# Layer 1's attention with its causal sum taken of the tokens, and one product for values and output

## The chip, the cores and the metric

The kernel runs on one core of one Trainium2 chip. The metric is device time in microseconds (us) of one execution, lower is better. TensorE is called PE below, VectorE DVE, ScalarE ACT, GpSimd POOL, and SyncE's queue SP.

## The reference, cut to what matters

The program is a small vision tower on 32 images of 256 tokens with 256 features: a tokenizer, layer 0 (gated attention, then a token-choosing feed-forward part), and layer 1 (the attention below, then a feed-forward part with heads and experts). The change touches only layer 1's attention and the preparation of its weights. Its input is a layer norm of the residual stream.

```python
def _L1_attn_ref(x, Wk1, bk1, Wk2, bk2, Wq1, bq1, Wq2, bq2, Wv, bv, ln_w, ln_b, Wo, bo):
    ...
    def encode(W1, b1, W2, b2):
        h = jax.nn.gelu(x @ W1 + b1, approximate=False)
        return jnp.tanh(h @ W2 + b2)
    key_phase = encode(Wk1, bk1, Wk2, bk2) * freq * jnp.pi
    query_phase = encode(Wq1, bq1, Wq2, bq2) * freq * jnp.pi
    key_phasor = jnp.cos(key_phase) + 1j * jnp.sin(key_phase)
    query_conj = jnp.cos(query_phase) - 1j * jnp.sin(query_phase)
    V = (x @ Wv + bv).astype(jnp.complex64)
    bound = key_phasor[..., None] * V[:, :, None, :]
    memory = jnp.cumsum(bound, axis=1)
    retrieved = jnp.real(jnp.sum(memory * query_conj[..., None], axis=2))
    positions = jnp.arange(1, Ll + 1, dtype=jnp.float32)
    retrieved = retrieved / jnp.sqrt(positions * K)[None, :, None]
    mu = jnp.mean(retrieved, axis=-1, keepdims=True)
    var = jnp.var(retrieved, axis=-1, keepdims=True)
    normed = (retrieved - mu) / jnp.sqrt(var + 1e-05) * ln_w + ln_b
    return x + normed @ Wo + bo
...
h = h + _L1_attn_ref(_layernorm(h, axis=-1), L1_attn_Wk1, ...)
```

The cumulative sum is the same as a causal match matrix (token against token, from the phases) times the values. Everything is float32.

## The kernel before, in words

The kernel goes through five stages, A to E: tokenizer (A), layer 0's attention (B), layer 0's feed-forward part (C), layer 1's attention (D), layer 1's feed-forward part (E). The residual stream of all images stays in SBUF, as 32 tiles `H[b]` of 128 partitions x 2 token blocks x 256 features. The eight PSUM banks are one pool; `bank()` takes the next of them, and a product into a bank waits until the bank's last reader has read it.

Stage D works on pairs of images, 16 pairs. Each pair goes through these steps, and three steps of time separate one pair from the next, so several pairs are under way at once:

- `norm`: two image tiles `dx` by DVE (line 172), four of them in turn; POOL adds `dx` and the row `add_row` to `H` (lines 623 and 624).
- `turn`: eight PE transposes of `dx` into two banks; ACT copies the first bank into `dxT`, DVE the second (`copy_split`, lines 191 and 193).
- `hidden`: for keys and for queries, four products of `wk1` or `wq1` with `dxT`, 512 columns each; ACT's gelu reads the bank (line 722).
- `phases`: the second layer into one bank, tanh (ACT), then range reduction on DVE into `dz`.
- `values_d`: eight products of `dxT` with `wv`, 256 columns each; DVE adds the bias row into `dv` (line 757).
- `match`: the sine (ACT), eight products of `dz`, and DVE multiplies with the causal weights into `dat` (line 777).
- `memory`: six products of `dat` with `dv`, 256 columns each; ACT copies them into `dr` (line 789); DVE takes mean and variance (`bn_stats` and `bn_aggr`, lines 792 and 793), and POOL makes the reciprocal deviation `d_rs` (`pow_rstd`, lines 146 and 147).
- `turn_back`: eight PE transposes of `dr`, copied into `drT` by ACT and DVE.
- `output`: eight products of `drT` with `wo1`, 256 columns each; DVE scales by `d_rs` and adds to `H` (line 813), and takes the statistics of `H` that stage E needs (lines 121 and 122).

In each step of time the steps that are due are written out in this order:

```python
ORDER = ((1, turn), (7, output), (4, match), (2, hidden), (5, memory), (3, phases), (6, turn_back),
         (3, values_d), (0, norm))
for t in range(3 * (B // 2 - 1) + 8):
```

So in the steady state PE's queue repeats, for each pair's period: match, hidden, memory, phases, turn_back, values_d, turn, output. A scheduler may move instructions against this order when the program is built, and each engine then works through its own queue in order. At step 21 `residuals` runs once: stage E's first products on images 0 to 3.

`prepare` runs once, in stage C, after its ninth step. It centres `wv` and the bias row (the reference's subtraction of the mean), makes `add_row` from `ln_b`, `Wo` and `bo`, multiplies `wo1` by `ln_w`, and makes stage E's weights. Its products stand in PE's queue between two of stage C's groups.

Of the kernel before, what the change touches and what calls it, by code (L numbers as in the profile page):

```python
# [29 lines left out]
F32 = mybir.dt.float32  # L33
AF = mybir.ActivationFunctionType
# [5 lines left out]
P = 128  # L40
# [38 lines left out]
def vit_tower(tc, a, out):  # L79
# [14 lines left out]
    def bank():  # L94
        return ppool.tile([P, 512], F32, name="bank", tag="bank")

    def col(name, i=0):
        c = COLS[name][0] + i
        return cols[:, c : c + 1]

    def load_rows(pool, name, at, n, eng=nc.scalar):

        t = pool.tile([P, n], F32, name=name)
        eng.dma_start(t, a[name].partition_broadcast(P))
        return lambda x: t[:, at[x][0] : at[x][0] + at[x][1]]

    def load(pool, name, eng=nc.scalar):
        t = pool.tile(list(a[name].shape), F32, name=f"w_{name}")
        eng.dma_start(t, a[name])
        return t  # L110
# [4 lines left out]
    def over(ap, shape, axis):  # L115
        return ap.unsqueeze(axis).to_broadcast(shape)
# [330 lines left out]
    pm = passing.enter_context(tc.tile_pool(name="e_made", bufs=1, side="right", reuse_waits="tile"))  # L447
    wk1, wq1 = load(pwd, "wk1", nc.sync), load(pwd, "wq1", nc.sync)
    wk2, wq2 = load(pwd, "wk2", nc.sync), load(pwd, "wq2", nc.sync)
    wv, wo1 = load(pwd, "wv1", nc.sync), load(pwd, "wo1", nc.sync)  # L450
    row_d = load_rows(pwd, "rows_d", ROWS_D, N_ROWS_D)
    causal = load(pwd, "causal_scaled", nc.sync)

    add_row = pwd.tile([P, D], F32, name="add_row")
    row_e = load_rows(pwe, "rows_e", ROWS_E, N_ROWS_E)
    hl, tri = load(pwe, "hl", nc.sync), load(pwe, "tri", nc.sync)
    cen, fg = load(pwe, "centre", nc.sync), load(pwe, "fg", nc.sync)
# [44 lines left out]
    def prepare():  # L502


        for w, g in ((wv, 2), (row_d("bv").unsqueeze(1), 1)):
            m = spool.tile([P, g], F32, name="d_mean", tag=f"d_mean{g}", bufs=1)
            nc.vector.tensor_reduce(m, w, AX.X, ALU.add)
            nc.vector.tensor_scalar(m, m, 1.0 / D, None, ALU.mult)
            nc.vector.tensor_tensor(w, w, over(m, [P, g, D], 2), ALU.subtract)
        p = bank()  # L510
        for k in range(2):
            mm(p[:, 0:D], col("ln_b", k).to_broadcast([P, P]), wo1[:, k, :], k == 0, k == 1)
        nc.vector.tensor_tensor(add_row, p[:, 0:D], row_d("bo"), ALU.add)
        for k in range(2):
            nc.vector.tensor_scalar(wo1[:, k, :], wo1[:, k, :], col("ln_w", k), None, ALU.mult)

        nc.gpsimd.memset(ones_row, 0.0)
        for o in (NE, EC + NE, 2 * EC + HD + NE, 3 * EC + HD + NE):
# [97 lines left out]
    def norm_d(b0, s, pool, name, bufs):  # L616
        s.xs = []
        for j in range(2):
            x = pool.tile([P, NC, D], F32, name=name, bufs=bufs)
            normed(x, b0 + j, st_d)  # L620
            s.xs.append(x)
            h = H[b0 + j]
            nc.gpsimd.tensor_tensor(h, h, x, ALU.add)
            nc.gpsimd.tensor_tensor(h, h, over(add_row, [P, NC, D], 1), ALU.add)
# [77 lines left out]
    with (  # L702
# [10 lines left out]

        def hidden(b0, s):
            s.g = []
            for i, (w, bias) in enumerate(((wk1, "bk1"), (wq1, "bq1"))):
                g = p2.tile([P, 2, 2 * N], F32, name=f"dg{i}")
                for m in range(2):
                    p = bank()
                    for k in range(2):  # L720
                        mm(p, w[:, k, m * P : (m + 1) * P], s.xT[:, k, :], k == 0, k == 1)
                    nc.scalar.activation(g[:, m, :], p, AF.Gelu, bias=col(bias, m))
                s.g.append(g)

        def phases(b0, s):
# [19 lines left out]
            nc.vector.tensor_scalar(n, z, MAGIC, MAGIC, ALU.add, ALU.subtract)  # L745
            nc.vector.tensor_sub(z, z, n)

        def values_d(b0, s):
            s.v = []
            for j in range(2):  # L750
                p = bank()
                for c in range(NC):
                    for k in range(2):
                        o = j * N + c * P
                        mm(p[:, c * D : (c + 1) * D], s.xT[:, k, o : o + P], wv[:, k, :], k == 0, k == 1)
                v = p8.tile([P, NC, D], F32, name="dv", bufs=6)
                nc.vector.tensor_tensor(
                    v, p.rearrange("p (c d) -> p c d", c=NC), over(row_d("bv"), [P, NC, D], 1), ALU.add
                )
                s.v.append(v)  # L760

        def match(b0, s):
            z = s.z.rearrange("p i n -> p (i n)")
            nc.scalar.activation(z, z, AF.Sin, scale=TWO_PI)
# [13 lines left out]
                s.t.append(t)  # L778

        def memory(b0, s):  # L780
            s.r = []
            s.st = spool.tile([P, 2 * NC, 2], F32, name="d_st")
            for j in range(2):
                t, v, p = s.t[j], s.v[j], bank()
                mm(p[:, 0:D], t[:, 0:P], v[:, 0, :])
                mm(p[:, D : 2 * D], t[:, P:N], v[:, 0, :], True, False)
                mm(p[:, D : 2 * D], t[:, N : N + P], v[:, 1, :], False, True)
                r = p8.tile([P, NC, D], F32, name="dr", bufs=4)
                nc.scalar.copy(r.rearrange("p c d -> p (c d)"), p)
                for c in range(NC):  # L790
                    six = spool.tile([P, 6], F32, name="six")
                    nc.vector.bn_stats(six, r[:, c, :])
                    nc.vector.bn_aggr(s.st[:, j * NC + c, :], six)
                s.r.append(r)
            s.rs = spool.tile([P, 2 * NC], F32, name="d_rs")
            pow_rstd(s.rs, s.st[:, :, 1])

        def turn_back(b0, s):
            s.rT = p2.tile([P, 2, 2 * N], F32, name="drT")
            transposed(s.rT, s.r, copy_split)  # L800

        def output(b0, s):
            for j in range(2):
                b = b0 + j
                p = bank()
                for c in range(NC):
                    for k in range(2):
                        o = j * N + c * P
                        mm(p[:, c * D : (c + 1) * D], s.rT[:, k, o : o + P], wo1[:, k, :], k == 0, k == 1)
                st, rs, i = at(st_e, b)  # L810
                for c in range(NC):
                    h, q = H[b][:, c, :], j * NC + c
                    nc.vector.scalar_tensor_tensor(
                        h, p[:, c * D : (c + 1) * D], s.rs[:, q : q + 1], h, ALU.mult, ALU.add
                    )
                    stats(st, i, c, h)
            pow_rstd_of(st_e, b0, 2)

        ORDER = ((1, turn), (7, output), (4, match), (2, hidden), (5, memory), (3, phases), (6, turn_back),
                 (3, values_d), (0, norm))
        for t in range(3 * (B // 2 - 1) + 8):
            if 1 <= t <= 3:
                step_c(END_C + t - 1)
            for at_step, do in ORDER:
                u, r = divmod(t - at_step, 3)
                if r == 0 and 0 <= u < B // 2:
                    do(2 * u, pairs[u])
            if t == 21:  # L830
                residuals(p2)
# [709 lines left out]
```

## Time and profile before

| what | value |
|---|---|
| three runs | 2065.7, 2072.34, 2075.61 us; median 2072.34 us |
| the profiled execution | 2072.35 us, of which the span from the first to the last instruction is 2070.5 us |
| mean granted PE clock | 0.978 of full speed |
| PE busy | 1984.3 us, 96% of the span |
| PE's weight loads | 1438.7 us, 69% |
| DVE busy | 1319.8 us, 64% |
| ACT busy | 829.6 us, 40% |
| POOL busy | 738.7 us, 36% |
| stage D | about 966 to 1340 us of the span |
| `prepare` on PE | 779.8 to 786.2 us |

The page divides the span in 40 slices of 51.8 us; stage D is slices 19 to 26. In the trace a float32 product of PE stands as two records, a transpose as one. Such records overlap: a 256-column record lasts 379 ns, but the next one starts 0.21 us after it. So starts are compared with starts here, not lengths.

### The profile page before, as it was taken

How to read it: one execution, taken by the hardware profiler on the slowest of the kernel's cores; microseconds unless marked ns; L12 is line 12 of the kernel's file. 1: busy time of each engine (PE TensorE's matmuls, PEld its weight loads, DVE VectorE, ACT ScalarE, POOL GpSimd, SP SyncE). 2: the span in 40 equal slices, each digit the busy share in tenths (PEclk: the TensorE clock that was granted, in tenths of full speed). 3: DMA queues.
4: the chain of work that ended last, by engine and by line, in shares of the span. 5: the costliest groups of instructions: out<-in, count | busy, mean ns of one | idle time of the engine just before them, and what ended most of it. 6: DMA issues, size and time to landing. Idle time of an engine off the chain costs nothing.

```text
span 2070.5 us, 38268 instructions
## 1 busy us (share of the span) xinstructions
PE 1984.3 (96%) x15406; PEld 1438.7 (69%) x15406; DVE 1319.8 (64%) x3589; ACT 829.6 (40%) x1569; POOL 738.7 (36%) x691
## 2 busy tenths in 40 slices
PE   8999999999999899998999999999999999999994
PEld 7886676666756656665666676677777777777772
DVE  3333557667575643335665565547888888888886
ACT  0001322222221021221433443367777777777762
POOL 2222224334242343336342332103444343444443
PEclk9999999999999999999999999989999999999996
DMA  8540000000000322212000000001222222121222
GB/s 273 153 145 0 1 0 21 13 19 18 13 21 11 127 81 72 74 53 58 1 1 1 1 1 1 1 19 35 53 48 56 50 49 57 43 61 45 58 50 55
DMA packets 69207, 95.12 MB, mean 46 GB/s; under 512 B 8480, under 2 KB 50592, under 8 KB 68640
## 3 DMA queue, kind: packets, MB, share of 16 engines
q1 hardware_dynamic: 62160, 74.33, 12.9%
q0 software_dynamic: 6144, 16.79, 2.8%
q8 instruction: 123, 2.02, 0.4%
q10 hardware_dynamic: 720, 1.50, 0.2%
q14 instruction: 60, 0.49, 0.1%
HBM read 46.45 MB, written 20.97 MB: 33 GB/s over the span
## 4 chain that ended last, share of the span: by engine, by line
PE 70%; DVE 20%; ACT 6%; DMA 2%; issue 2%; POOL 1%; SPq 0%; DVEq 0%; ACTq 0%; POOLq 0%
PE bank L113 66%; DVE bank L932 4%; ACT et L934 2%; PE bank L186 2%; DVE ranges L1025 1%; DVE two L1017 1%; ACT g L892 1%; DVE fout L1095 1%; DVE fout L1091 1%; DVE ev L905 1%; ACT foT L1078 1%; DVE er L1019 1%; DVE enorm L1066 1%; PE bank L583 1%; DVE ey L1058 1%
## 5 line engine op out<-in xcount | busy, mean ns | idle before, releaser
L113 PEld LDWEIGHTS bank<-ev,et 128*64 128x64 f32 x6144 | 198.2, 137 | 34.0 <-ACT et L934 21.7
L934 ACT ACTIVATE et<-bank 128x512 f32<-128x512 f32 x384 | 202.4, 598 | 34.8 <-DVE bank L932 34.1
L113 PE MATMUL bank<-ev,et 128*64 128x74 f32 (+1 forms) x6144 | 211.2, 226 | 0.0
L1012 POOL TENSOR_TENSOR eo<-eo,gate 128x1024 f32<-128x1024 f32 x64 | 131.5, 2074 | 204.7 <-DVE gate L1009 156.7
L932 DVE TENSOR_TENSOR bank<-bank,w_tri 128x256 f32<-128x256 f32 (+1 forms) x384 | 172.0, 515 | 30.2 <-PE bank L113 29.5
L113 PE MATMUL bank<-g,sx 64*128 64x512 f32 (+1 forms) x512 | 186.6, 506 | 1.4 <-ACT g L892 1.4
L113 PE MATMUL bank<-g,sw 64*128 64x512 f32 (+1 forms) x512 | 185.5, 507 | 1.4 <-DVE ev L905 1.4
L113 PE MATMUL bank<-w_tokW,patch 128*128 128x256 f32 x768 | 169.0, 384 | 9.3 <-DMA w_tokW<-in_tokW_dram 9.3
L113 PEld LDWEIGHTS bank<-w_tokW,patch 128*128 128x128 f32 x768 | 148.0, 193 | 30.0 <-issue 9.3
L113 PE MATMUL bank<-bxT,w_wuv 128*128 128x512 f32 x320 | 147.9, 601 | 4.3 <-ACT bxT L191 4.0
L191 ACT COPY bxT<-bank 128x512 f32<-128x512 f32 x16 | 9.4, 585 | 339.2 <-PE bank L186 339.2
L964 POOL TENSOR_TENSOR hv<-hv,minus_half 128x8 f32<-128x8 f32 x64 | 119.5, 1868 | 5.3
L950 ACT COPY eo<-bank 128x286 f32<-128x286 f32 x256 | 97.2, 422 | 48.7 <-PE bank L113 40.9
L113 PE MATMUL bank<-w_w,hT 128*128 128x256 f32 x512 | 114.5, 383 | 0.0
L963 POOL TENSOR_SCALAR hv<-ranges 128x8 f32<-128x8 f32 x64 | 38.8, 606 | 210.8 <-DVE ranges L1025 210.8
L113 PE MATMUL bank<-xsel,w_w 128*128 128x512 f32 x256 | 113.5, 600 | 0.0
L113 PE MATMUL bank<-attn,bv 128*128 128x256 f32 x512 | 113.3, 379 | 0.0
L113 PE MATMUL bank<-w_wo,gT 128*128 128x256 f32 x512 | 113.1, 379 | 0.0
L113 PE MATMUL bank<-w_wuv,bxT 128*128 128x512 f32 x256 | 112.5, 592 | 0.0
L113 PEld LDWEIGHTS bank<-attn,bv 128*128 128x128 f32 x512 | 97.1, 190 | 19.5 <-issue 6.7
L113 PEld LDWEIGHTS bank<-w_w,hT 128*128 128x128 f32 x512 | 97.9, 192 | 16.8 <-issue 3.8
L113 PEld LDWEIGHTS bank<-w_wo,gT 128*128 128x128 f32 x512 | 97.3, 190 | 13.2
(241 smaller groups left out, 3968.8 us busy)
## 6 DMA issues: line engine op xcount, KB each, us to landing
patch<-in_patches_dram SPq DMA_DIRECT2D x32, 768.0 KB, 4.6
sw<-sx SPq DMA_DIRECT2D x64, 128.0 KB, 2.4
both<-fxT SPq DMA_DIRECT2D x64, 128.0 KB, 2.4
both<-hx SPq DMA_DIRECT2D x64, 128.0 KB, 2.3
out_dram<-fout SPq DMA_DIRECT2D x32, 256.0 KB, 2.5
cs<-ranked SPq DMA_DIRECT2D x32, 128.0 KB, 3.4
results<-cy SPq DMA_DIRECT2D x32, 128.0 KB, 1.8
w_w<-in_w_dram SPq DMA_DIRECT2D x2, 1024.0 KB, 6.8
```

The lines of the kernel that those rows point to most:

```text
L113: nc.tensor.matmul(o, lhsT, rhs, start=first, stop=last)
L186: nc.tensor.transpose(p[:, o : o + P], x[:, c, k * P : (k + 1) * P], ident)
L583: nc.tensor.transpose(p[:, o : o + P], x[:, c, k * P : (k + 1) * P], ident)
L892: nc.scalar.copy(im.g[:, 2 * hp + h, :, :].rearrange("p j n -> p (j n)"), p)
L905: nc.vector.tensor_tensor(im.v.rearrange("p c (k h) x -> p (c k) h x", h=2)[:, :, h, :], p[:, 0 : 2 * NC * VC].rearrange("p (g x) -> p g x ...
L932: nc.vector.tensor_tensor(own, own, over(tri, [P, n_e, P], 1), ALU.add)
L934: nc.scalar.activation(t, p, AF.Exp)
L950: nc.scalar.copy(im.o[:, c * NH + n, 0:OC], p[:, 0:OC])
L963: nc.gpsimd.tensor_scalar(v, x, 1.0 / HD, 1e-8, ALU.mult, ALU.add)
L964: nc.gpsimd.tensor_tensor(v, v, minus_half, ALU.pow)
L1012: nc.gpsimd.tensor_tensor(im.mix[k], im.mix[k], over(im.gate[:, :, 2 * k : 2 * k + 2], [P, NC * NH, 2, HD], 3), ALU.mult)
L1017: nc.vector.tensor_tensor(two, im.mix[0], im.mix[1], ALU.add)
```

## The change

The causal sum is linear, so it can be taken of the tokens before the values' weights are applied: `dat` times `dx` in place of `dat` times `dv`. What remains is a product with the values' weights (wanted for the variance) and one with values' by output's weights (wanted for the result). The two matrices lie side by side in one tile `wvo` of 512 columns, so one product gives both.

- `values_d` and `turn_back` go, with `dv`, `dr` and `drT`.
- `memory` makes the sum transposed, features on partitions: per image two products of 256 columns and two of 128, in turn, with `dx` as the weights. ACT copies it to `dm`. It reads `s.xs`, so the `dx` tiles are in use until then.
- `output` makes eight products of 512 columns, into four banks. DVE takes mean and variance from the first half of each bank, POOL makes the reciprocal deviation from all four, and then DVE scales the second half of each bank and adds it to `H`. It now stands one step earlier, at 6, before `norm` and ahead of the next step's `turn`.
- The value bias has to come out of the sum. A constant row is added to each token for that (`norm_d` writes tokens plus one, `(x - mean) * rstd + 1`), with the weights adjusted so that the column sums of `wv` equal the bias; the first layers' biases (`bias_d`) and `add_row` are corrected for the added one.
- `prepare` gets the products for these column sums, four transposes of `wv`, and the four products of values' by output's weights, with DVE's steps between them. `ones_d` is set by POOL.

```diff
-    wv, wo1 = load(pwd, "wv1", nc.sync), load(pwd, "wo1", nc.sync)
+    wvo = pwd.tile([P, 2, 2 * D], F32, name="wvo")
+    wv = wvo[:, :, 0:D]
+    nc.sync.dma_start(wv, a["wv1"])
+    wo1 = load(pwd, "wo1", nc.sync)
...
     def prepare():
...
+        ones_d = pm.tile([P, P], F32, name="ones_d")
+        nc.gpsimd.memset(ones_d, 1.0)
         p = bank()
         for k in range(2):
             mm(p[:, 0:D], col("ln_b", k).to_broadcast([P, P]), wo1[:, k, :], k == 0, k == 1)
-        nc.vector.tensor_tensor(add_row, p[:, 0:D], row_d("bo"), ALU.add)
+        q = bank()
         for k in range(2):
+            mm(q[:, 0:D], ones_d, wv[:, k, :], k == 0, k == 1)
+        for i, w in enumerate((wk1, wq1)):
+            for m in range(2):
+                o = D + 2 * i + m
+                for k in range(2):
+                    mm(q[:, o : o + 1], w[:, k, m * P : (m + 1) * P], ones_d[:, 0:1], k == 0, k == 1)
+        nc.vector.scalar_tensor_tensor(add_row, p[:, 0:D], -1.0, row_d("bo"), ALU.add, ALU.add)
+        c = COLS["bk1"][0]
+        nc.vector.tensor_tensor(bias_d, cols[:, c : c + 4], q[:, D : D + 4], ALU.subtract)
+        u = row_d("bv")
+        nc.vector.tensor_tensor(u, u, q[:, 0:D], ALU.subtract)
+        for k in range(2):
+            nc.vector.scalar_tensor_tensor(wv[:, k, :], u, 1.0 / D, wv[:, k, :], ALU.mult, ALU.add)
             nc.vector.tensor_scalar(wo1[:, k, :], wo1[:, k, :], col("ln_w", k), None, ALU.mult)
+        p = bank()
+        for m in range(2):
+            for k in range(2):
+                o = m * D + k * P
+                nc.tensor.transpose(p[:, o : o + P], wv[:, k, m * P : (m + 1) * P], ident)
+        wvT = pm.tile([P, 2, D], F32, name="wvT")
+        nc.vector.tensor_copy(wvT.rearrange("p m d -> p (m d)"), p)
+        p = bank()
+        for k in range(2):
+            for m in range(2):
+                mm(p[:, k * D : (k + 1) * D], wvT[:, m, k * P : (k + 1) * P], wo1[:, m, :], m == 0, m == 1)
+        nc.vector.tensor_copy(wvo[:, :, D:], p.rearrange("p (k d) -> p k d", k=2))
...
     def norm_d(b0, s, pool, name, bufs):
...
-            normed(x, b0 + j, st_d)
+            st, rs, i = at(st_d, b0 + j)
+            q = slice(i * NC, (i + 1) * NC)
+            one = spool.tile([P, NC], F32, name="d_one")
+            nc.vector.scalar_tensor_tensor(one, st[:, i, :, 0], -1.0, rs[:, q], ALU.mult, ALU.mult)
+            nc.vector.tensor_scalar(one, one, 1.0, None, ALU.add)
+            for c in range(NC):
+                nc.vector.tensor_scalar(
+                    x[:, c, :], H[b0 + j][:, c, :], rs[:, i * NC + c : i * NC + c + 1], one[:, c : c + 1],
+                    ALU.mult, ALU.add,
+                )
...
         def memory(b0, s):
-            s.r = []
-            s.st = spool.tile([P, 2 * NC, 2], F32, name="d_st")
+            s.m = []
             for j in range(2):
-                t, v, p = s.t[j], s.v[j], bank()
-                mm(p[:, 0:D], t[:, 0:P], v[:, 0, :])
-                mm(p[:, D : 2 * D], t[:, P:N], v[:, 0, :], True, False)
-                mm(p[:, D : 2 * D], t[:, N : N + P], v[:, 1, :], False, True)
...
-        def turn_back(b0, s):
...
+                t, x, p = s.t[j], s.xs[j], bank()
+                for k in range(2):
+                    o, d = k * N, slice(k * P, (k + 1) * P)
+                    mm(p[:, o : o + N], x[:, 0, d], t[:, 0:N], True, False)
+                    mm(p[:, o + P : o + N], x[:, 1, d], t[:, N : N + P], False, True)
+                m = p8.tile([P, 2, N], F32, name="dm", bufs=4)
+                nc.scalar.copy(m.rearrange("p k n -> p (k n)"), p)
+                s.m.append(m)
 
         def output(b0, s):
...
+            st_m = spool.tile([P, 2 * NC, 2], F32, name="d_st")
+            ps = []
+            for q in range(2 * NC):
+                m, c, p = s.m[q // NC], q % NC, bank()
+                for k in range(2):
+                    mm(p, m[:, k, c * P : (c + 1) * P], wvo[:, k, :], k == 0, k == 1)
+                six = spool.tile([P, 6], F32, name="six")
+                nc.vector.bn_stats(six, p[:, 0:D])
+                nc.vector.bn_aggr(st_m[:, q, :], six)
+                ps.append(p)
+            rs_m = spool.tile([P, 2 * NC], F32, name="d_rs")
+            pow_rstd(rs_m, st_m[:, :, 1])
+            for q, p in enumerate(ps):
+                b, c = b0 + q // NC, q % NC
+                st, _, i = at(st_e, b)
+                h = H[b][:, c, :]
+                nc.vector.scalar_tensor_tensor(h, p[:, D:], rs_m[:, q : q + 1], h, ALU.mult, ALU.add)
+                stats(st, i, c, h)
             pow_rstd_of(st_e, b0, 2)
...
-        ORDER = ((1, turn), (7, output), (4, match), (2, hidden), (5, memory), (3, phases), (6, turn_back),
-                 (3, values_d), (0, norm))
-        for t in range(3 * (B // 2 - 1) + 8):
+        ORDER = ((1, turn), (4, match), (2, hidden), (5, memory), (3, phases), (6, output), (0, norm))
+        for t in range(3 * (B // 2 - 1) + 7):
```

## The prediction

> **What bounds the kernel now.** I read the page first: it shows PE as the busiest engine, and its row by slices shows it full through stage D (slices 19 to 26, counted from 0).
>
> ```profile
> PE 1984.3 (96%) x15406; PEld 1438.7 (69%) x15406; DVE 1319.8 (64%) x3589; ACT 829.6 (40%) x1569; POOL 738.7 (36%) x691
> PE   8999999999999899998999999999999999999994
> PE 70%; DVE 20%; ACT 6%; DMA 2%; issue 2%; POOL 1%; SPq 0%; DVEq 0%; ACTq 0%; POOLq 0%
> ```
>
> A busy share is an average, so next comes the chain of waits for 1044 to 1112 us: it has only PE in it. In steady D, then, PE's own issue sets the time, and starts on PE's timeline give each step's price:
>
> ```profile
> 1093.29 1.09 PE L186 MATMUL bank<-ident,dr 128*128 128x128 f32 x8
> 1094.22 3.62 PE L113 MATMUL bank<-w_wv,dxT 128*128 128x256 f32 x16
> 1097.68 1.04 PE L186 MATMUL bank<-ident,dx 128*128 128x128 f32 x8
> 1098.55 3.62 PE L113 MATMUL bank<-w_wo,drT 128*128 128x256 f32 x16
> 1102.10 1.58 PE L113 MATMUL bank<-dz 64*128 64x256 f32 x16
> 1103.61 3.70 PE L113 MATMUL bank<-dxT,w_wk 128*128 128x512 f32 x8
> ```
>
> Start to start: turn_back 0.93, values 3.46, turn 0.87, output 3.55, match 1.51; the next group of `hidden` starts at 1107.14, so 8 records of 512 columns take 3.53. One pair's period is 21.85.
>
> Then I read DVE and POOL around `d_rs`, because the change puts them between PE's groups:
>
> ```profile
> 1168.57 0.19 POOL L146 TENSOR_SCALAR d_rs<-d_st 128x4 f32<-128x4 f32 x1 [8.36 <-DVE d_st L793]
> 1168.85 1.01 POOL L147 TENSOR_TENSOR d_rs<-d_rs,minus_half 128x4 f32<-128x4 f32 x1
> ...
> 1174.36 0.69 DVE L193 COPY dxT<-bank 128x512 f32<-128x512 f32 x1
> ...
> 1176.89 0.86 DVE L813 SCALAR_TENSOR_TENSOR h<-bank,d_rs,h 128x256 f32<-128x256 f32 x2
> ```
>
> `d_rs` was ready at 1169.86 and is used at 1176.89: it has 7 us to spare, and the copy of `dxT` stands ahead of its user.
>
> The granted clock by microseconds, last, around a wait of 2.6 us at D's start:
>
> ```profile
> 990.00:991.00 1.00, 0.00 (x0) 0.00 (x0) 1.00 (x4) 0.99 (x2) 0.03 (x1) 1.00 0.00 0
> 991.00:992.00 1.00, 0.78 (x6) 0.72 (x8) 1.00 (x2) 0.98 (x2) 1.00 (x1) 0.87 0.00 0
> 992.00:993.00 1.00, 1.00 (x8) 0.83 (x8) 0.49 (x1) 0.47 (x1) 0.92 (x2) 0.50 0.00 0
> ```
>
> The third figure from the end is the clock: it falls to half just after PE resumes, and is back in the slice of 995.
>
> **What the Trainium skill says.** "PSUM — Partial Sum Buffer", section Engine vs sequencer instructions: ScalarE's, VectorE's and GpSimdE's queues are strict FIFO. The trace agrees: no DVE instruction here overtakes an earlier one that waits, and my main step rests on it. "TensorE: Matmul & The Clock Gate", Part 1, The HAM clock gate: PE's clock drops to half after an idle window of about 3.4 us, windows running free. Half speed and length agree (some 3.2 us at 0.50 here); the idle needed doesn't: waits of 1.95 (783.1 to 785.0) and 2.6 us were followed by half speed, one of 1.5 (1120.1 to 1121.6) wasn't. "Perfetto Trace Analysis", section Matmuls: larger matmuls are more efficient when possible. Between 256 and 512 columns the trace disagrees: 3.46/16 = 0.216 us a record against about 0.436 for twice the columns.
>
> **The change part by part.**
>
> PE work per pair. Removed: turn_back 0.93, values 3.46, output 3.55, together 7.94. Added: 8 products of 512 columns, 16 records at 0.436 (mean of `hidden`'s groups of 8, 3.53 and 3.44) = 6.97. So the fused product saves no columns (8 x 512 against 16 x 256); only the transposes go. Memory keeps 1536 columns, but 8 products in place of 6: before, 12 records in 2.68, 0.223 each; after, 8 of those and 8 of 128 columns, at about 0.12 (the 64-column records of L113 `w_hl,exT` start 0.119 apart, transposes of 128 columns 0.11), 2.75: +0.07. Net -0.90 a pair, times 16 = **-14.4**.
>
> The new wait. In the compiled program's queues PE runs output, turn, match, then `hidden`; its first two products need ACT's half of `dxT` only, the third needs DVE's half. DVE's queue has this copy behind the whole tail of output: four statistics, then (after POOL) four scalings and four statistics of `H`. All that is after output's last product. From PE's first transpose of turn (0):
>
> - last product's data 0.16 (a 512-column record lasts 0.592, the next starts 0.43 after), hand-over 0.09 (1327.91 to 1328.00): 0.25
> - `bn_stats` 0.42 and `bn_aggr` 0.17: 0.84
> - POOL: 0.09 + 0.19 + 0.09 + 1.01 = 1.38: 2.22; back to DVE 0.09: 2.31
> - the same scalings and statistics in the same order ran once before, at the end of D: 1339.14 to 1342.24, 3.10: 5.41
> - the copy 0.69, hand-over 0.04: 6.14
>
> PE arrives at 0.87 + 1.51 + 4 x 0.436 = 4.12. It waits 2.02, with everything of `hidden` and later behind it. Outputs 0 to 13 are followed by a `hidden`; after output 5 `residuals` stands between (10 us of PE), which covers it. So 13 waits, **+26.3**. ACT's gelu, waiting on PE, only shifts.
>
> `prepare`. Its PE work is 4 records of 256 columns and 16 of one column (`w_fg,cols`, 4 columns: about 0.1 each), 4 transposes, 8 records: 0.86 + 1.6 + 0.5 + 1.7 = 4.7. PE's queue has them in one piece, with DVE between: the bias steps wait behind an update of `H` whose data came at 783.64; they, one `bn_stats` and two scalings of `wv` end near 785.9; transposes to 786.3; the copy `wvT` behind another update, near 787.5; four products to 789.2; then stage E's weights as before (1.9), and their copies. The group that started at 785.03 starts near 791.9: **+6.9**. The chain of waits is PE alone from 785 to 955, so it is paid in full; cover there would bring it to 0, more updates ahead of the two copies to 10.
>
> D's start. Values of pair 0 (3.46, credited above) covered the sine of `match`, which ended at 991.18. Without them it comes about 1.3 earlier, the chain tanh, DVE, table load, sine remaining: **+2.2** (0 to 3.5).
>
> D's end. Waits were 0.78 + 0.24 + 0.51 + 2.44 = 3.97. After, match (15) ends at 1.51 and memory waits for `dat`, behind the same scalings, to 6.1, 4.6 us; E's first transposes then wait for nothing. **+0.7** (-3 to 3).
>
> Costed at nothing: four `d_one` steps a pair (DVE has 26 to 33 of 50 us in D's windows) and ACT's and DVE's lost copies. `dx` tiles are held until memory, so `norm` writes after it, some 7 us ahead of turn; were that cover gone, turn would wait for up to four writes, 2.4 us. The four banks: `hidden`'s second product takes the first of them, free after the first scaling at 2.8, reached at 3.3. POOL's adds to `H` end before the next `d_rs`; beneath them DVE's range reduction may run slower, hidden under output's 7 us. SP gets the same loads.
>
> The clock. No wait of 2.0 us stands in the trace; those on both sides differ. Free windows of 3.4 us catch some of the waits whole. A half-speed window costs half of some 3.3 us, 1.65; from 0 to all 13 that is 0 to 21. I take four: **+6.6**.
>
> Sum: -14.4 + 26.3 + 6.9 + 2.2 + 0.7 + 6.6 = +28.3, on the profiled execution's 2072.35 (span 2070.5 and 1.85 around it), the same as the median of 2072.34: 2100.6, so 2100.
>
> **The rivals.**
> *The copy comes in time.* If DVE's part is done when PE needs it, the 26.3 and 6.6 go: 2072.35 - 14.4 + 6.9 + 2.2 + 0.7 = 2068, no change; with `prepare` covered as well 2061, faster. For it: ACT makes half of `dxT` early, and DVE has idle time. Against it: idle time doesn't help a queue that waits for POOL. It decides at the wait's length: all else as above, (14.4 - 9.8)/13 = 0.35 us a pair breaks even, 1.15 makes it slower by 10.4 us (0.5%, about what a measurement here can tell from no change).
> *The clock falls after every wait.* 13 x 1.65 in place of 6.6: 2115. For it: 1.95 us sufficed in `prepare`, where the products were tiny; against it: around our wait they are dense, and windows can split it.
> *The saving isn't what it says.* Were 512 columns cheaper than twice 256, PE would gain more; `hidden`'s own records say no. At 0.42, which is below any group of them here, -4 us.
>
> **How the numbers follow.** The copy in time: 0.17 (no change 0.10, faster 0.07). Clock after every wait: 0.17. The main case 0.63, 0.02 of it within 0.5%. The rest, a cheaper product with covered preparation, 0.03 (0.02 no change, 0.01 faster). Faster 0.08, same 0.14, slower 0.78. The waits' reading may err by 0.5 us, 6.5 in all; with the clock's ends and `prepare`'s the main case has 2084 to 2120. Down to 2072 it takes in part of the first rival, and 2124 lets the second pay a little more: 2072 to 2124.
>
> **What would show it.** In PE's timeline, `hidden` splits after four records, with about 2 us idle put down to DVE's `dxT`; the period is near 23 us; `wvo,dm` takes 7.0 for 16 records. No such idle would refute the main step, a period under 21.5 with it. `prepare`'s last group should start 7 us after where it did, and slices of half clock in D count the clock's share.

## The result, and the profile after

The changed kernel takes 2096.22 us (median of four runs, 2094.23 to 2100.5) against 2072.89 for the kernel before (four runs, 2065.7 to 2075.61). The ratio is 1.0121, 95% interval 1.009 to 1.0151: 1.2% slower. The forecast was 2100, in a range of 2072 to 2124. The profiled execution took 2097.27 us (span 2095.5), 24.9 more than that of before, with a mean clock of 0.974.

The page of the changed kernel: its busy row, its row of slices for PE, and the shares of the chain that ended last.

```profile
PE 1984.1 (95%) x15118; PEld 1392.4 (66%) x15118; DVE 1347.5 (64%) x3611; ACT 823.6 (39%) x1553; POOL 742.0 (35%) x692
PE   8999999999999899998999999899999999999994
PE 66%; DVE 23%; ACT 6%; DMA 2%; issue 2%; POOL 1%; SPq 0%; DVEq 0%; ACTq 0%; POOLq 0%
```

PE's busy total is almost what it was (1984.3): the work that goes in stage D, the work that `prepare` gains and more time at half speed about cancel in it, so that row alone says nothing. The chain says more: DVE's share of it went from 20% to 23%, PE's from 70% to 66%. For one pair of stage D the PE timeline shows where (start, length, group, and in brackets the idle time before it and its releaser):

```profile
1012.52 7.13 PE L114 MATMUL bank<-wvo,dm 128*128 128x512 f32 x16
1019.49 1.04 PE L187 MATMUL bank<-ident,dx 128*128 128x128 f32 x8
1020.46 1.58 PE L114 MATMUL bank<-dz 64*128 64x256 f32 x16
1021.96 1.98 PE L114 MATMUL bank<-dxT,w_wk 128*128 128x512 f32 x4
1025.57 1.98 PE L114 MATMUL bank<-dxT,w_wk 128*128 128x512 f32 x4 [1.62 <-DVE dxT L194]
...
1035.41 7.13 PE L114 MATMUL bank<-wvo,dm 128*128 128x512 f32 x16
```

`output` takes 6.97 start to start. `hidden` is split after its fourth record, and PE stands 1.62 us until DVE has copied `dxT`. The period is 22.89 in place of 21.85. What PE waits for can be followed in the chain of waits of the same stretch (start, length, what ran):

```profile
1019.69 0.44 DVE six L832
...
1020.71 1.03 POOL d_rs L148
1021.73 0.03 issue
1021.76 0.88 DVE h L841 x2
...
1024.94 0.58 DVE dxT L194
1025.53 0.04 issue
1025.57 10.54 PE bank L114 x45
```

In before's steady D the chain was PE alone. Here, for some 6 us of each period, it runs through `output`'s tail: the last `bn_stats`, POOL's `d_rs`, DVE's scalings with their statistics, and only then the copy. The list of PE's waits over D (total, times, longest) has this wait on top:

```profile
PE bank L114 <- DVE dxT L194: 24.5, 14, 3.4
PE bank L114 <- ACT dz L795: 6.3, 1, 6.3
PE bank L114 <- DVE dat L808: 4.3, 1, 4.3
```

One of the 14, of 3.4 us, stands at D's start and was there before. The other 13 are the pairs' and last 1.62 us each. The idle column counts from the modelled end of the last record; by starts a pair loses 1.89, as the first experiment's period shows.

The clock in windows of 1 us (third figure from the end), around a wait of a pair and in `residuals`:

```profile
1024.00:1025.00 1.00, 0.00 (x0) 0.00 (x0) 1.00 (x5) 0.00 (x0) 0.00 (x0) 1.00 0.00 0
1025.00:1026.00 1.00, 0.43 (x1) 0.30 (x2) 1.00 (x4) 0.00 (x0) 0.22 (x2) 1.00 0.00 0
1026.00:1027.00 1.00, 1.00 (x4) 0.42 (x3) 0.51 (x2) 0.27 (x1) 0.98 (x1) 1.00 0.00 0
...
1138.00:1139.00 1.00, 1.00 (x8) 1.00 (x7) 1.00 (x6) 0.00 (x0) 0.00 (x0) 0.57 0.00 0
1139.00:1140.00 1.00, 0.70 (x4) 0.30 (x2) 1.00 (x7) 0.20 (x1) 0.00 (x0) 0.50 0.00 0
```

The clock stayed full after each of the 13 waits. It fell in `residuals`, from 1138.14 to 1151.78, where the prediction had not looked for it. Half speed lasts 3.4 us or a multiple of it in these traces (3.42, 6.83 and 13.66 us in the experiments below); a stretch of 3.4 us is called a window here, so these are four windows. In the kernel before, the same groups with waits of the same length had full speed throughout:

```profile
1123.00:1124.00 1.00, 0.32 (x3) 0.15 (x2) 0.80 (x3) 0.59 (x1) 0.00 (x0) 1.00 0.00 0
```

Last, `prepare` on PE:

```profile
775.68 1.03 PE L114 MATMUL bank<-w_wo,cols 128*128 128x256 f32 x4
...
781.09 1.24 PE L544 MATMUL bank<-ident,wvo 128*128 128x128 f32 x4 [1.84 <-DVE wvo L538]
783.11 3.68 PE L114 MATMUL bank<-w_wo,wvT 128*128 128x256 f32 x8 [0.78 <-DVE wvT L546]
...
790.92 1.95 PE L679 MATMUL bank<-ident,cs 128*128 128x128 f32 x8
```

It lasts 15.24 us from the first group to stage C's next transposes, 6.36 before. Its last products run at half speed, 8 records in 3.61. The clock fell at 779.7, some 0.5 us after PE had come to the first of the two waits, behind products of one column.

By stages, from starts on PE in the two profiled executions:

| stretch | before | after | difference |
|---|---|---|---|
| up to stage C's steady part | 751.42 | 747.26 | -4.2 |
| rest of stage C, with `prepare` | 213.93 | 224.02 | +10.1 |
| D's start: turn (0) to match (0) | 25.87 | 26.23 | +0.4 |
| match (0) to match (15) | 338.33 | 355.92 | +17.6 |
| D's end: match (15) to E's first transposes | 13.21 | 17.11 | +3.9 |
| stage E | 727.74 | 724.96 | -2.8 |

The first row is taken as no effect of the change: that part of the program is the same, and in the traces of the ten experiments below, which have it too, this point lies anywhere from 745.9 to 751.1. In the last row, E's first products ran at half speed for 13.7 us before, and for 3.4 after.

### The profile page after: what moved, and what is told of

It reads as the page before. It is cut to its first block, busy times and chain, and to the rows that moved or that the text cites. A ratio compares the mean times of both kernels' runs of the same rounds, so it can differ in the third digit from the quotient of the medians.

```text
span 2095.5 us, 37669 instructions
## 1 busy us (share of the span) xinstructions
PE 1984.1 (95%) x15118; PEld 1392.4 (66%) x15118; DVE 1347.5 (64%) x3611; ACT 823.6 (39%) x1553; POOL 742.0 (35%) x692
## 4 chain that ended last, share of the span: by engine, by line
PE 66%; DVE 23%; ACT 6%; DMA 2%; issue 2%; POOL 1%; SPq 0%; DVEq 0%; ACTq 0%; POOLq 0%
PE bank L114 64%; DVE bank L957 4%; ACT et L959 2%; DVE ranges L1050 1%; DVE two L1042 1%; ACT g L917 1%; DVE h L841 1%; DVE six L122 1%; DVE fout L1120 1%; DVE fout L1116 1%; DVE ev L930 1%; PE bank L619 1%; ACT foT L1103 1%; DVE er L1044 1%; DVE enorm L1091 1%
## 5 line engine op out<-in xcount | busy, mean ns | idle before, releaser
L114 PE MATMUL bank<-wvo,dm 128*128 128x512 f32 x256 | 114.0, 598 | 0.0
```

Source lines behind the costliest of these rows:

```text
L114: nc.tensor.matmul(o, lhsT, rhs, start=first, stop=last)
```

## The experiments

Ratios are to the kernel before, on the same chip; the changed kernel's is 1.0121.

### Both copies on ACT

```diff
-            transposed(s.xT, s.xs, copy_split)
+            transposed(s.xT, s.xs, lambda k, o, p: nc.scalar.copy(o, p))
```

> The changed kernel, but in turn both halves of dxT are copied by ACT, so that no copy stands in DVE's queue behind output's tail. Theory (the copy's place in DVE's queue makes the wait): the idle of 1.62 us ahead of hidden's third product goes in all 13 pairs, the period falls from 22.89 to 21.0, and the time from 2096 by 13 x 1.87 = 24 to about 2072, the time of the kernel before. Rival 1 (the banks: hidden's products wait for banks that the scalings hold, whoever copies dxT): the period stays near 22.9 and the time within 3 us of 2096. Rival 2 (ACT becomes late: two copies of 0.6 one after the other ahead of its gelu): a new wait of about 0.5 us a pair, 2078.

Measured: 2071.38 us, ratio 0.9984 (0.9976 to 0.9993). PE's timeline of this kernel:

```profile
1062.69 1.04 PE L187 MATMUL bank<-ident,dx 128*128 128x128 f32 x8
1063.66 1.58 PE L114 MATMUL bank<-dz 64*128 64x256 f32 x16
1065.16 3.70 PE L114 MATMUL bank<-dxT,w_wk 128*128 128x512 f32 x8
...
1083.69 1.04 PE L187 MATMUL bank<-ident,dx 128*128 128x128 f32 x8
```

`hidden` is whole again, and the period is 21.00. So the wait cost 22.89 - 21.00 = 1.89 us a pair. The banks, which this edit doesn't touch, held nothing up, and ACT's second copy came in time. From match (0) to match (15), the first and the last pair's match, this trace takes 332.39, 23.5 less than the changed kernel's.

### Output behind turn

```diff
-        ORDER = ((1, turn), (4, match), (2, hidden), (5, memory), (3, phases), (6, output), (0, norm))
-        for t in range(3 * (B // 2 - 1) + 7):
+        ORDER = ((1, turn), (7, output), (4, match), (2, hidden), (5, memory), (3, phases), (0, norm))
+        for t in range(3 * (B // 2 - 1) + 8):
```

> The changed kernel, but output stands where it stood before the change, one step later and behind turn; DVE still copies its half of dxT. Theory (queue order): DVE's copy now comes ahead of output's statistics and scalings, and output's 7 us on PE cover it; hidden waits for nothing, the period is 21.0 and the time about 2072. DVE's tail of 6 us then lies under match and hidden (8.5 us), so that dat isn't late. Rival 1 (DVE's tail only moves the wait, to memory's wait for dat): 1 to 2 us idle in front of memory in each pair, 2085 to 2096. Rival 2 (banks: match and hidden wait for banks that output's scalings hold): as much idle at match or hidden, 2085 or more.

Measured: 2072.38 us, ratio 0.9997 (0.9989 to 1.0005). Neither rival showed: no wait at match, hidden or memory is left in the steady part, and the period is 21.32 (hidden's starts at 1065.45 and 1086.77), a little longer than above because turn ahead of `output` takes 1.28. DVE still makes its copy, only earlier in its queue. With the first experiment this shows that the copy's place behind `output`'s tail made the wait, and not DVE's load.

### Statistics twice

```diff
                 stats(st, i, c, h)
+                stats(st, i, c, h)
```

> The changed kernel, but output takes the statistics of H twice after each scaling (the second time with the same result): four bn_stats and four bn_aggr more in DVE's queue ahead of the copy of dxT. By starts one such pair costs 0.37 + 0.09 = 0.46 us. Theory: the wait in front of hidden's third product grows by 4 x 0.46 = 1.8 us in 13 pairs, 24 us, to about 2120. If the clock also fell after waits of that length (3.4 us idle), up to 13 x 1.65 = 21 us more, 2141. Rival (DVE has idle time, and PE's period is set by something else): no change, 2096.

Measured: 2093.95 us, ratio 1.0103 (1.0081 to 1.0125): no slower than the changed kernel. The rival's number is the nearer one, and the theory's missed by 26 us. The timelines tell why. DVE's copy did move: it starts at 1068.12, 6.94 us after turn's first transpose at 1061.18, in the changed kernel 5.37. But PE's queue isn't the same either:

```profile
1063.66 1.98 PE L114 MATMUL bank<-dxT,w_wk 128*128 128x512 f32 x4
1065.48 1.92 PE L114 MATMUL bank<-dxT,w_wq 128*128 128x512 f32 x4
1068.83 1.98 PE L114 MATMUL bank<-dxT,w_wk 128*128 128x512 f32 x4 [1.43 <-DVE dxT L194]
```

The scheduler, which builds each queue, put the queries' first four records ahead of the products that wait. The copy came 1.57 us later (6.94 less 5.37), these records fill 1.76 of it, and the old wait of 1.62 becomes 1.62 + 1.57 - 1.76 = 1.43, which is what the trace shows. So this run agrees with the mechanism, but it isn't the test that it was meant to be: an edit on DVE changed PE's order. The next test writes that order on purpose.

### First halves first

```diff
-            for i, w in enumerate((wk1, wq1)):
-                ...
-                for m in range(2):
-                    p = bank()
-                    for k in range(2):
-                        mm(p, w[:, k, m * P : (m + 1) * P], s.xT[:, k, :], k == 0, k == 1)
+            ps = [bank() for _ in range(4)]
+            for k in range(2):
+                for q, p in enumerate(ps):
+                    w, m = (wk1, wq1)[q // 2], q % 2
+                    mm(p, w[:, k, m * P : (m + 1) * P], s.xT[:, k, :], k == 0, k == 1)
...
```

> The changed kernel, but hidden takes its eight products in another order: first the four (two for keys, two for queries) that need only the half of dxT that ACT copies, then the four that need DVE's half. Nothing else moves; DVE's queue is as it was. In the changed kernel DVE's copy is done 6.04 us after turn's first transpose. Theory (PE stands only for that copy): PE reaches the first product that needs it at 0.97 + 1.51 + 8 records x 0.436 = 5.97 in place of 4.2, so 0.1 us of the 1.87 is left, the period falls from 22.89 to 21.1 and the time by 13 x 1.77 = 23 to about 2073. Rival 1 (banks: the third and fourth bank come free with the third and fourth scaling only, at 4.2 and 4.7, and products ask for them at 4.2 and 5.1): up to 0.5 us of the wait stays, 2080. Rival 2 (DVE's lag itself sets the period, wherever PE waits for it): the idle moves behind hidden, to memory's wait for dat, 2096.

Measured: 2071.82 us, ratio 0.9994 (0.9985 to 1.0004).

```profile
1060.71 1.04 PE L187 MATMUL bank<-ident,dx 128*128 128x128 f32 x8
1061.67 1.58 PE L114 MATMUL bank<-dz 64*128 64x256 f32 x16
1063.18 1.98 PE L114 MATMUL bank<-dxT,w_wk 128*128 128x512 f32 x4
1065.00 1.88 PE L114 MATMUL bank<-dxT,w_wq 128*128 128x512 f32 x4
1066.79 1.98 PE L114 MATMUL bank<-dxT,w_wk 128*128 128x512 f32 x4
```

No idle is left, and the period is 21.17 (next turn at 1081.88), where 21.1 was worked out. DVE's queue is as late as in the changed kernel; PE merely asks for its half 1.8 us later, and the wait's price is gone in full.

### Residuals spread

`residuals` in five parts: one image's transposes at the end of a step, its products at the end of the next, on top of both copies on ACT.

```diff
-            if t == 21:
-                residuals(p2)
+            if 22 <= t < 22 + NH:
+                residual(p2, t - 22, turned)
+            if 21 <= t < 21 + NH:
+                turned = residual_turned(p2, t - 21)
```

> The kernel with both copies on ACT (ratio to before 0.9984), with one more edit: residuals spread over five steps, one image's transposes in one step, its products in the next. In the changed kernel and in this one's parent the clock is at half for 13 us from residuals on (four windows of some 3.3), in before never there, though residuals issues the same groups with waits of the same length. Theory A (the chain of small groups and waits lets the clock fall, by the place of free-running windows): with products of other steps between them it stays full, and 6.6 us of clock and 2.9 us of idle go, ratio 0.994. Theory B (the fall there has another cause): the idle alone goes, ratio 0.997.

Measured: 2061.81 us, ratio 0.9941 (0.992 to 0.9962), as theory A said. In the trace, match (0) to match (15) takes 321.40, 11.0 less than in the first experiment, and after the first pairs no window of half speed is left between them. Written as one block, the same groups had half speed for four windows in the changed kernel, in the first experiment and in the two kernels below that have the block with `prepare` in three parts, for two in "statistics twice" and "first halves first", for one in "output behind turn", for none before. What the block does to the clock thus varies between kernels. That it depends on where windows begin, which no edit here sets, is consistent with this, but was not tested by itself.

### Prepare in three parts

```diff
+            if t == 6:
+                prepare_sums()
+            if t == 7:
+                prepare_turned()
             if t == 8:
                 prepare()
```

The first part goes up to the scaling of `wo1`, the second holds the transposes of `wv` and the copy `wvT`, the third the rest.

> The changed kernel, but prepare is cut in three: the column sums and corrections come two steps of stage C earlier, the transposes of wv one step earlier, and the product of values' by output's weights stays with the rest. In the changed kernel prepare's waits on DVE (1.84 for wvo, 0.78 for wvT) and the half clock around them stand on PE's path. Theory (the waits and the clock are a part of prepare's cost, some 6 us): these waits are filled by stage C's own products, and of about 6 us only the added PE work of 4 to 5 us, less what is hidden, stays: 2 to 4 us faster, 2092 to 2094. Rival (the cost is PE work alone, or the waits come back at the next place): within 1 us of 2096.

Measured: 2093.56 us, ratio 1.0092 (1.0067 to 1.0117). That interval overlaps the changed kernel's, so the trace has to decide: the rest of stage C takes 217.97 there, against 224.02 (changed) and 213.93 (before). So 6.1 of the 10.1 us went, more than the 2 to 4 expected, and 4.0 are left, about the added PE work. What went is put down to the waits and the half speed around them, by the sum and not by a run that takes one away without the other.

### Another order, and all together

Prepare in three parts, with match behind hidden and the sine as a step of its own:

```diff
-        ORDER = ((1, turn), (4, match), (2, hidden), (5, memory), (3, phases), (6, output), (0, norm))
-        for t in range(3 * (B // 2 - 1) + 7):
+        ORDER = ((1, turn), (4, sine), (7, output), (2, hidden), (5, match), (3, phases), (6, memory), (0, norm))
+        for t in range(3 * (B // 2 - 1) + 8):
```

> Prepare in three parts as in the run before, and another order of stage D: turn, sine (its own step), output (one step later, behind turn), hidden, match (one step later, behind hidden), phases, memory, norm. So output's 7 us on PE cover the copies of dxT, hidden's 7 us cover the sine and DVE's tail, and phases covers dat. Theory: no wait in the steady period, 21.0; at D's start match (0) stands behind hidden (1) and the 6 us wait for the sine goes. From the three-part run (2093.5): 24 for the waits and 6 for the start, 2063 to 2066, ratio to before 0.996. Rival (ACT or DVE, with the sine and gelu closer together, now comes late for match, phases or output): a new wait of 0.5 us or more a pair, 2072 or more.

Measured: 2080.74 us, ratio 1.0041 (1.003 to 1.0052): of the 30 us expected, 11 (by the ratios) to 13 (by the medians) came. PE's timeline around turn:

```profile
1064.99 2.88 PE L114 MATMUL bank<-dat,dx 128*128 128x256 f32 x16
...
1070.63 0.33 PE L187 MATMUL bank<-ident,dx 128*128 128x128 f32 x1 [0.60 <-DVE dx L667]
1071.97 0.55 PE L187 MATMUL bank<-ident,dx 128*128 128x128 f32 x3 [1.01 <-DVE dx L667]
```

`memory` now stands straight ahead of `turn`, so the `dx` tiles that it lets go are written only then, and turn waits for the writes, 19.3 us over D. That is about what is missing. That is the case that the prediction had costed at nothing for the changed kernel, with its cover named (memory some 7 us ahead of turn). Neither the theory nor the rival of this run had thought of it.

Next, the same order with three edits more: copies on ACT, residuals spread, and the transposes of `wv` and the product of values' by output's weights moved to D's first two steps, with their copies on ACT:

```diff
-            if t == 7:
-                prepare_turned()
...
+            if t == 1:
+                prepare_turned()
+            if t == 2:
+                prepare_product()
             if 1 <= t <= 3:
                 step_c(END_C + t - 1)
```

> The order of the kernel just above, with three more edits: both halves of dxT copied by ACT; the transposes of wv and the product of values' by output's weights taken at D's start, where PE stands some 6 us in front of hidden (0); and residuals spread over five steps, one image's transposes in one step and its products in the next. Theory: 2.3 us for the PE work moved into a gap, some 2 for the copies at D's start, 3 us of idle in residuals, and up to 6.6 us for the four half-speed windows there: 2050 to 2058, ratio 0.990 to 0.993. Rival (what hidden (0) waits for is ACT's queue, into which two more copies now go, and half-speed windows come elsewhere): no more than the idle in residuals, 2061 to 2066.

Measured: 2067.81 us, ratio 0.9967 (0.9956 to 0.9979). What was expected of it was written before the result of its parent, the kernel just above, was known, so the same wait for `dx` (19.8 us) is in it and in no number of its expectation. The moved products did find their gap: the rest of stage C takes 215.35, 8.7 less than in the changed kernel, and hidden (0) then waits 0.41 us.

The wait for `dx` puts a price on its tiles, so the next kernel has six of them in place of four.

> The kernel with all edits together (ratio 0.9967), with six dx tiles in place of four. In that kernel and its parent turn waits for norm's dx in 12 pairs, 0.6 + 1.0 = 1.6 us each, because the new order puts memory, which reads the dx of an earlier pair, straight ahead of turn, and norm can write only into tiles that memory has let go. Theory (the tiles are what norm waits for): with two more tiles norm writes a pair earlier, the waits go, the period falls from 22.9 to 21.0, and 19 to 20 us go: 2048, ratio 0.987 to 0.988. Rival (norm waits for DVE's own queue, behind output's scalings, or for H): the waits stay, 2066.

```diff
-                norm_d(b0, s, p8, "dx", 4)
+                norm_d(b0, s, p8, "dx", 6)
```

Measured: 2050.2 us, ratio 0.9887 (0.9868 to 0.9907).

```profile
1066.82 1.04 PE L187 MATMUL bank<-ident,dx 128*128 128x128 f32 x8
1067.69 7.03 PE L114 MATMUL bank<-wvo,dm 128*128 128x512 f32 x16
1074.56 3.60 PE L114 MATMUL bank<-dxT,w_wk 128*128 128x512 f32 x8
```

The waits for `dx` are gone, and the period is 20.81 (from 1053.75 to 1074.56, hidden's starts). The gain over the kernel with all edits together, 0.8% or 17 us, is a little short of the 19 to 20 expected: at D's start, match (0) now waits 8.7 us for the sine, 3.3 in that kernel, because norm writes a pair more there, in DVE's queue ahead of the range reduction.

The last kernel goes back to the changed kernel's order and four tiles, and keeps the other edits.

> All edits together, but with the changed kernel's order of stage D (output at 6, ahead of turn; match at 4, ahead of hidden; memory ahead of phases) and four dx tiles. Theory: memory stands 9 us ahead of turn again, so turn waits for no dx, and with ACT's copies hidden waits for nothing; what the other order brings at D's start (match (0) waits 3.3 us there, 7 to 9 in the old order) is lost. From the spread residuals (0.9941) less 9 us for prepare out of the path: 2051 to 2054, ratio 0.989 to 0.991. Rival (the transposes and products moved to D's start delay hidden (0), and the sine's wait grows by as much as they save): 2057 or more.

```diff
-        ORDER = ((1, turn), (4, sine), (7, output), (2, hidden), (5, match), (3, phases), (6, memory), (0, norm))
-        for t in range(3 * (B // 2 - 1) + 8):
+        ORDER = ((1, turn), (4, sine), (4, match), (2, hidden), (5, memory), (3, phases), (6, output), (0, norm))
+        for t in range(3 * (B // 2 - 1) + 7):
```

Measured: 2053.51 us, ratio 0.9913 (0.9889 to 0.9936), as the theory said. Yet what the rival named is in the trace too: match (0) waits 10.5 us for the sine, where the theory had 7 to 9. The interval overlaps that of six `dx` tiles: the other order as such brought nothing that these runs can tell. Both kernels keep the fused product and beat both originals, by about 1% the kernel before and 2% the changed one. No run gave the kernel before the same edits (`residuals` spread above all), so these figures are not the worth of the fused product alone; that is read from the period, 0.85 us a pair.

## Why the prediction was right, and where not

**PE's work per pair: right.** 0.90 less was worked out. Without the wait the period is 21.00 against 21.85: 0.85 less. `output` measures 6.97, as predicted; turn takes 0.97 behind its 512-column groups, 0.87 before, and memory 2.71 where 2.75 was worked out, which together is the missing part. The third rival (a cheaper product) is out.

**The new wait: right in place, near in size.** The chain from turn's first transpose came out as follows: `d_rs` ready at 2.24 (predicted 2.22), scalings at 2.27 (2.31), the copy's start at 5.37 (5.41), PE released at 6.08 (6.14). PE's arrival was put at 4.12 and lies at 4.21: the slower turn again. So 1.89 us a pair were lost where 2.02 were predicted, 24.6 us in all for 26.3. What the Trainium skill says in "PSUM — Partial Sum Buffer", section Engine vs sequencer instructions, on which the step rested (DVE's queue is strict FIFO), agrees with the traces: in the changed kernel and in each of the three experiments that leave `output`'s tail ahead of DVE's copy ("statistics twice", "first halves first", `prepare` in three), this copy started at least 0.65 us after its pair's last scaling had ended, in the changed kernel 4.3 us after turn's last transpose; and "output behind turn" moved its place in the queue and with it the wait. The first rival, that the copy comes in time, is refuted by the changed kernel and made true by the first two experiments.

**`prepare`: right in kind, too small.** +6.9 was predicted, with 10 as the upper end; stage C paid 10.1. The PE work was near (4.7 worked out, 4.0 left in three parts). What the sum left out was the clock: its waits of 1.84 and 0.78 us stand among tiny products, and half speed came with them, four windows (779.7 to 786.6 and 790.0 to 796.8) where the kernel before had one: 1.9 us more for the last products and 1.2 in stage C's groups behind them. The prediction had seen this in the kernel before (1.95 us of idle there, then half speed) and priced it only in D.

**D's start: too small.** +2.2 was predicted beside values' 3.46. The stretch got 0.4 longer although these 3.46 are gone: +3.8, a little above its own upper end of 3.5. The sine came no earlier without values (match (0) starts 9.3 us after phases (0), 9.1 before), so PE waits 6.34 us for it, 2.61 before. DVE's timeline shows where the 1.3 us went by which it should have come earlier. These are the first two steps of the range reduction for pair 0, before and after:

```profile
985.07 1.04 DVE L742 TENSOR_SCALAR dz<-dturn,cols 128x512 f32<-128x512 f32 x2 [1.12 <-ACT dturn L740]
991.12 2.79 DVE L787 TENSOR_SCALAR dz<-dturn,cols 128x512 f32<-128x512 f32 x2 [0.57 <-ACT dturn L785]
```

From the first step to the last, range reduction took 5.24 us in place of 3.98. POOL was adding to `H` from 990.97 to 993.63, just while the two steps took 2.79. The prediction had named this slowing and put it at nothing, as hidden under `output`'s 7 us. In the later pairs it is hidden (these steps take 1.88 there), but for pair 0 no `output` stands in PE's queue yet.

**D's end: near.** By the prediction's own terms the stretch grows by 2.5 of work, 0.1 of memory and 0.7 of waits; it grew by 3.9. One window of half speed, in which memory took 4.40 in place of 2.7, more than accounts for the other 0.6.

**The clock: right sum, wrong place.** Four half-speed windows after the 13 waits, 6.6 us, were taken as the likeliest. After these waits there was none, so the second rival (2115) was further off still. There were four windows in `residuals` in their stead. From one pair's match to the next, the period with this block takes 36.63, 13.74 more than a period with a wait; before it took 31.68, 9.83 more than 21.85. The next period, whose wait the block covers as predicted, takes 22.47 in place of 21.00, its start still at half speed. So the four windows cost 3.9 + 1.5 = 5.4. A sum that comes out by such an exchange is luck in this term. Around a pair's wait PE runs 512-column products without a gap; in `residuals` it has waits of some 0.7 us between small groups, and in the changed kernel that was worse than one wait of 1.9. The Trainium skill's "TensorE: Matmul & The Clock Gate", Part 1, has the clock drop after an idle window of about 3.4 us; in `residuals` no idle was longer than 0.73, and the measurement decides.

So match (0) to match (15) is 15 x (-0.85) + 13 x 1.89 + 5.4 = 17.2; the first period, at half speed in both kernels, adds 0.3 (22.95 is 1.95 above 21.00, before 23.48 was 1.63 above 21.85), and the table shows 17.6. With stage C's 10.1, D's ends of 0.4 and 3.9, the 2.8 by which stage E was shorter (it starts with three windows of half speed fewer) and 4.2 of difference ahead of stage C's steady part, that makes the 25.0 us of the spans; the medians lie 23.3 apart. The forecast was +28.3. Term by term the runs differ from it by +0.7 (work), -1.7 (wait), +3.2 (`prepare`), +1.6 and +0.6 (D's start and end), -0.8 (clock, with the first period), and by the two rows that it didn't count, -2.8 and -4.2: together -3.4, which leads from 28.3 to 25.0 but for rounding. Without these two rows the sum would have been 3.6 above the forecast, so that the total came so near is in part luck.

## What to carry to other kernels

When a step that ends on another engine is moved ahead of a step that needs that engine, read that engine's queue in order: what counts is what stands ahead of the one instruction that is waited for, not the engine's idle time. Such a wait can be taken away without making the late engine faster, and each of three ways did it here: give the copy to another engine, let PE do first what needs only the half that is there, or put the copy ahead of the long tail. Before a step that reads a tile is put straight ahead of the step that needs the tile's next contents, count the tiles.

## What the hardware showed that was not expected

**The clock fell without a long idle.** A run of small groups with waits of 0.7 us each had half speed for up to four windows, and for none in the kernel before. In `prepare` it fell some 0.5 us after PE had stopped behind products of one column. Single waits of 1.6 us among 512-column products had no half speed behind them in any of 13 cases.

**One of DVE's smallest steps took as long as POOL's addition beside it.** The four `d_one` steps of a pair were put at nothing, and they stayed hidden, but in most pairs not because they are short. The list of instructions on this tile in the changed kernel (durations in ns: least, median, most):

```profile
L659 DVE SCALAR_TENSOR_TENSOR d_one<-st_d,rs_d x32: 146/160/1105, 758.0 to 1298.3; 128x2 f32<-128x2 f32 x32
L660 DVE TENSOR_SCALAR d_one<-d_one x32: 127/1142/1148, 758.2 to 1298.5; 128x2 f32<-128x2 f32 x32
```

The second step works on two elements a partition. It takes 0.13 us at best, and 1.14 at the median. One pair's steps, with POOL's addition beside them:

```profile
1033.15 1.27 POOL L668 TENSOR_TENSOR h<-h,dx 128x512 f32<-128x512 f32 x1 [6.17 <-DVE dx L662]
1033.30 1.15 DVE L660 TENSOR_SCALAR d_one<-d_one 128x2 f32<-128x2 f32 x1
```

POOL's addition starts 0.15 us before the second step and ends at 1034.42, the step at 1034.45. So it is in all 23 of these steps from 1033 us on: each ends 0.02 to 0.03 us after the addition beside it. Two that ran beside POOL's power step (128 x 4) instead took 0.15 and 0.17. The Trainium skill's "SBUF — State Buffer", section SBUF: two separate sides, says that VectorE and GpSimd share a pair of ports as an exclusive lock, which whichever starts first holds for its whole instruction while the other fully blocks, when the VectorE instruction runs in a mode that takes both of its ports or reads two operands from SBUF. The ends of the steps fit that; whether the second step runs in such a mode the traces don't say, and no run took POOL's additions away to prove it.
